# The bias of the own products as a row product on TensorE, and their copy on ScalarE, in the norm stage of a graph and mixture-of-experts kernel

## The chip, the cores and the metric

The kernel runs on one core of a Trainium2 chip. The core has five engines that run their own instruction queues in order: TensorE (PE in the profile, with its weight loads apart as PEld), VectorE (DVE), ScalarE (ACT), GpSimd (POOL) and SyncE (SP, which here only issues transfers). Sixteen DMA engines move data between HBM and the on-chip memory SBUF; matrix products land in PSUM, from which another engine must copy them. The metric is the time of one execution on the device in microseconds (us). Of several executions the median is compared.

## The reference, cut to what matters

```
x = x + gnn(layernorm(x), src, dst, W_self1, W_neigh1, b1, W_self2, W_neigh2, b2)
x = x + moe(layernorm(x), Wg, W1, b1, W2, b2, gamma, beta)

def sage_layer(h, src, dst, W_self, W_neigh, b):
    agg = segment_sum(h[src], dst, n_nodes)
    deg = segment_sum(ones, dst, n_nodes)
    return relu(h @ W_self + (agg / max(deg, 1)) @ W_neigh + b)
```

The graph part is two such layers over 6250 nodes of 512 floats and 100000 edges sorted by target. The mixture-of-experts part picks 2 of 8 experts for each node. Everything is float32. What the change touches is one term of the first layer: `h @ W_self1 + b1`, with h the normed rows; below it is called the own product, and `b1` (the argument `gb1` of the kernel) its bias, a row of 512 numbers.

## The kernel before

Nodes are cut into 49 blocks of 128 rows (the last has 106). The kernel runs in stages: the norm stage (the first 117 us), the first layer with its edge sums, the second layer with its routing, and the experts' end. The edge sums gather rows of the normed matrix `xn_d` from HBM by GpSimd's indirect transfers (`gather`, L216), and the first gather has to wait until the last block is normed and stored.

The norm stage is one loop of 54 steps over k (from L505 on), in an order written out by hand: PE, DVE, ACT and POOL execute their instructions in exactly the order in which the program issues them. In step k:

- `stats` of block k: row statistics on DVE (L460, L462), then a square root on ACT (L464).
- `add_bias` in steps 14, 17, 20, ...: DVE adds the bias, spread over 128 rows in `bb1`, to the own product made five steps before, out of PSUM (L494).
- `nearly`, in steps 9 to 23: DVE copies a turned table of edge indices out of PSUM (L152), whose transposition PE did in the step before.
- `norm` of block k-1: DVE takes the reciprocal and scales the rows (L472, L473), SP stores them to `xn_d` (L476), and PE transposes them into one of three PSUM tiles `pt` (four transposes, L480).
- `turn_edges`, in steps 8 to 22: DVE casts an index table to float (L149) and PE transposes it (L151).
- `keep` of block k-4: ACT copies the transposed block out of PSUM into the resident table `big` (L484). This frees the `pt` tile that `norm` of the same step wants.
- `own` in steps 9, 12, 15, ..., 45 (13 of them): four float32 products of a kept block with `ws1` into a PSUM tile `pm`, of which there are three (L489; the profile counts two passes for each product, so 8).

The own products of the other 36 blocks are made later, in the first layer (`u0`, L561), and are not touched. Their bias is still `bb1`.

GpSimd's queue in this stage holds, in this order: the loads of the edge indices (L141, L143), the experts' rows (`experts_rows`, L380), two small stores, and then the gathers. `experts_rows` loads `b1`, then handles `b2`, `gamma` and `beta` of the experts one after the other: it splits each 8x512 table into three bf16 parts whose sum is the float32 value (load L386, cast L389, store L390, cast back L393, subtract L394) and loads the stored parts again as 24 rows (L395). Each step of this waits for the one before it, since the queue is in order.

Of the kernel before, what the change touches and what calls it, by code (L numbers as in the profile page):

```python
# [29 lines left out]
F32 = mybir.dt.float32  # L30
I32 = mybir.dt.int32
U32 = mybir.dt.uint32
BF16 = mybir.dt.bfloat16
# [16 lines left out]
def bcast(ap, n):  # L50

    return bass.AP(tensor=ap.tensor, offset=ap.offset, ap=[[0, P], [1, n]])
# [15 lines left out]
def gnn_moe(ctx, tc, x, src, dst, Ws1, Wn1, gb1, Ws2, Wn2, gb2, Wg, W1, b1, W2, b2, gamma, beta, out):  # L68
    nc = tc.nc
    N, D = x.shape  # L70
    E = src.shape[0]
    NE = Wg.shape[1]
    C = D // P
# [12 lines left out]
    dram = ctx.enter_context(tc.tile_pool(name="dram", bufs=1, space=DRAM))  # L86
# [20 lines left out]
    ones_h = consts.tile([P, P], BF16, name="ones_h")  # L107
# [218 lines left out]
    def part(i):  # L326
        return big[:, i * D : (i + 1) * D]
# [49 lines left out]
    pick_e = rt.tile([NP3, NE], F32, name="pick_e")  # L377
    thirds = {name: rt.tile([NP3, D], BF16, name=f"{name}_3") for name in ("b2", "gamma", "beta")}

    def experts_rows(pool, psp):  # L380
        b1r = pool.tile([NE * HC, P], F32, name="b1r")
        nc.gpsimd.dma_start(b1r, b1.rearrange("e (c p) -> (e c) p", p=P))
        for name, ap in (("b2", b2), ("gamma", gamma), ("beta", beta)):
            to = dram.tile([NE, 3, D], BF16, name=f"{name}_d")
            left = pool.tile([NE, D], F32, name=f"left_{name}")
            nc.gpsimd.dma_start(left, ap)  # L386
            for k in range(3):
                h = pool.tile([NE, D], BF16, name=f"h_rows{k}")
                nc.gpsimd.tensor_copy(h, left)  # L389
                nc.gpsimd.dma_start(to[:, k], h)  # L390
                if k < 2:
                    f = pool.tile([NE, D], F32, name="f_rows")
                    nc.gpsimd.tensor_copy(f, h)  # L393
                    nc.gpsimd.tensor_sub(left, left, f)  # L394
            nc.gpsimd.dma_start(thirds[name], to.rearrange("e k d -> (e k) d"))  # L395
        lo = pool.tile([NP3, NE], F32, name="lo")
        nc.vector.tensor_scalar(lo, iota_row[:NP3, :NE], 3.0, iota_p[:NP3], op0=OP.mult, op1=OP.subtract)
        hi = pool.tile([NP3, NE], F32, name="hi")
        nc.vector.tensor_scalar(hi, lo, -3.0, None, op0=OP.is_gt)
        nc.vector.tensor_scalar(lo, lo, 0.0, None, op0=OP.is_le)  # L400
        nc.vector.tensor_mul(pick_e, lo, hi)

        def turn():
            pt = psp.tile([P, P], F32, name="pd")
            nc.tensor.transpose(pt[:, : NE * HC], b1r, ident[: NE * HC, : NE * HC])
            nc.vector.tensor_copy(b1T, pt[:, : NE * HC])

        return turn
# [7 lines left out]
    xnT = [part(b).rearrange("p (c n) -> p c n", c=C) for b in range(NB)]  # L416
# [3 lines left out]
    def load_w(w, name):  # L420
        t = lay.tile([P, C, D], F32, name=name)
        nc.scalar.dma_start(t, w.rearrange("(c p) f -> p c f", p=P))
        return t

    def load_b(b, name):
        t = lay.tile([P, D], F32, name=name)
        nc.scalar.dma_start(t, bcast(b, D))
        return t

    with tc.tile_pool(name="l0", bufs=3, side="right") as pool, \  # L430
            tc.tile_pool(name="prep", bufs=1, side="right") as prep, \
            tc.tile_pool(name="l0p", bufs=2, space=PSUM) as psp:

        batch = []
        for lo, hi in ((NS, NB), (0, NS)):
            full = hi if rows[hi - 1] == P else hi - 1
            at = lo
            while at < full:
                batch.append((at, min(4 if batch else 1, full - at)))
                at += batch[-1][1]  # L440
            batch += [(b, 1) for b in range(full, hi)]
        order = [b0 + t for b0, m in batch for t in range(m)]
        at_batch = {b0: i for i, (b0, m) in enumerate(batch)}
        stores = {b0 + m - 1: (b0, m) for b0, m in batch[:-1]}
        stores.update({b: (b, 1) for b in range(batch[-1][0], sum(batch[-1]))})
        where, spread, turned, made = {}, {}, {}, []

        def load(i):
            if i < len(batch):
                b0, m = batch[i]  # L450
                n = rows[b0]
                xt = pool.tile([P, 4, D], F32, name="xt")
                xn = pool.tile([P, 4, D], F32, name="xn")
                nc.sync.dma_start(xt[:n, :m], x[b0 * P : b0 * P + m * n].rearrange("(t p) d -> p t d", p=n))
                where.update({b0 + t: (xt[:, t], xn, t) for t in range(m)})

        def stats(b):
            n = rows[b]
            st = pool.tile([P, 6], F32, name="st")
            nc.vector.bn_stats(st[:n], where[b][0][:n])  # L460
            mv = pool.tile([P, 2], F32, name="mv")
            nc.vector.bn_aggr(mv[:n], st[:n])  # L462
            rs = pool.tile([P, 1], F32, name="rs")
            nc.scalar.activation(rs[:n], mv[:n, 1:2], AF.Sqrt, bias=eps[:n], scale=1.0)  # L464
            spread[b] = mv, rs

        def norm(b):
            n = rows[b]
            mv, rs = spread.pop(b)
            xt, xns, t = where.pop(b)  # L470
            xn = xns[:, t]
            nc.vector.reciprocal(rs[:n], rs[:n])  # L472
            nc.vector.tensor_scalar(xn[:n], xt[:n], mv[:n, 0:1], rs[:n], op0=OP.subtract, op1=OP.mult)  # L473
            if b in stores:
                b0, m = stores[b]
                nc.sync.dma_start(xn_d[b0 * P : b0 * P + m * n].rearrange("(t p) d -> p t d", p=n),  # L476
                                  xns[:n, t + 1 - m : t + 1])
            turned[b] = psp.tile([P, C, P], F32, name="pt", bufs=3)
            for c in range(C):
                nc.tensor.transpose(turned[b][:, c, :n], xn[:n, c * P : (c + 1) * P], ident[:n, :n])  # L480

        def keep(b):
            n = rows[b]
            nc.scalar.activation(xnT[b][:, :, :n], turned.pop(b)[:, :, :n], AF.Copy)  # L484

        def own(b):
            ps = psp.tile([P, D], F32, name="pm", bufs=3)
            for c in range(C):
                nc.tensor.matmul(ps, xnT[b][:, c], ws1[:, c], start=(c == 0), stop=(c == C - 1))  # L489
            made.append((b, ps))  # L490

        def add_bias():
            b, ps = made.pop(0)
            nc.vector.tensor_add(part(b), ps, bb1)  # L494

        load(0)
        load(1)
        dT = prep.tile([P, NCH * TS], F32, name="dT")
        nearly = None
        NE1 = NB - NS  # L500
        when = [9 + j * (NB - 9) // NE1 for j in range(NE1)]
        with tc.manual_schedule(engines=HAND):


            for k in range(NB + 5):  # L505
                if k < NB:
                    if order[k] in at_batch:
                        load(at_batch[order[k]] + 2)
                    stats(order[k])
                if k == 0:  # L510

                    nc.gpsimd.tensor_copy(tick, spread[order[0]][0][:1, :1])
                    raws = load_edges(prep)
                    ws1 = load_w(Ws1, "ws1")
                    bb1 = load_b(gb1, "bb1")
                    turn_b1 = experts_rows(prep, psp)
                    edges_for_loops(prep)
                if k == NB // 2:
                    wn1 = load_w(Wn1, "wn1")
                if k - 5 in when:  # L520
                    add_bias()
                if nearly:
                    nearly()
                    nearly = None
                    if not raws:
                        edge_tables(prep, psp, dT)
                if 0 <= k - 1 < NB:
                    norm(order[k - 1])
                if k >= 8 and raws:
                    nearly = turn_edges(prep, psp, dT, *raws.pop(0))  # L530
                if k == NB // 2:
                    turn_b1()
                if 0 <= k - 4 < NB:
                    keep(order[k - 4])
                if k in when:
                    own(order[when.index(k)])
            while made:
                add_bias()

    lay = b_ctx.enter_context(tc.tile_pool(name="lay2", bufs=1, side="left"))  # L540
    wn2, ws2 = (lay.tile([P, C, D], F32, name=name) for name in ("wn2", "ws2"))
# [358 lines left out]
    with tc.tile_pool(name="s2", bufs=2, side="right") as pool, \  # L900
# [3 lines left out]
        own = {}  # L904
# [295 lines left out]
    def slow_path(pool, psp):  # L1200
# [68 lines left out]
        def spread(name, ap):  # L1269
            t = pool.tile([P, D], F32, name=name)  # L1270
            nc.sync.dma_start(t, bcast(ap, D))
            return t

        def layer(own, wn, ws, bb, b, n, last):
            r = bass.ds(b * P, n)
            a = load_rows("now", agg, r, n)
# [95 lines left out]
```

## Time and profile before

| what | value |
|---|---|
| median of 3 runs | 3350.38 us (3343.76 to 3356.97) |
| the profiled execution | 3328.7 us, its span 3326.4 us |
| busy over the span: PE, DVE, ACT, POOL | 2694.6, 1346.4, 691.5, 1846.9 us |
| mean granted TensorE clock | 0.894 |
| first gather of the first layer (L220) | starts at 117.45 us |
| 20 to 40 us: PE, DVE, ACT busy | 14.23, 12.74, 4.42 us of 20 |
| 80 to 100 us: PE, DVE, ACT busy | 20.00, 19.15, 9.58 us of 20 |
| L494, the addition of the bias | 13 times, 8.6 us in all, 660 ns each |
| L489, the own products | 104 passes, 53.7 us in all |
| L484, ACT's copy of a transposed block | 48 full ones, 27.4 us in all |

The profile shows one execution. A line of its timelines gives the start in us, the length in us, the engine and the line of the program, the operation, the output and the inputs, and how many such instructions were merged into the line; a bracket at its end tells how long the engine had been idle before and what released it. "MATMUL" durations overlap: the next product starts before the one before it has ended.

The span is an unbroken sequence of stages, so what lengthens or shortens the norm stage moves everything behind the first gather.

### The profile page before, as it was taken

To read this page: it belongs to the slowest core of one execution; us is meant where nothing else is said; L and a number is where in the kernel's file an instruction comes from. 1 tells how busy PE (TensorE), PEld (TensorE's weight loads), DVE (VectorE), ACT (ScalarE), POOL (GpSimd) and SP (SyncE) were. 2 spreads that over 40 slices of the span, in tenths; PEclk is the share of its full clock that TensorE was granted. 3 is DMA by queue.
4 is the path that set the end of the run, shared out by engine and by line. 5 is a ranking of instruction groups with operands and counts; after the bars stand their busy time and mean duration, and the time that the engine had idled before them with its cause. 6 is when DMAs were issued, how large, how long until landed. Compare 5 with 4: busy or idle time off the path is not lost. (4 is left out here: it accounts for less than half of the span.)

```text
span 3326.4 us, 34415 instructions
## 1 busy us (share of the span) xinstructions
PE 2694.6 (81%) x10010; PEld 1075.8 (32%) x10010; DVE 1346.4 (40%) x4313; ACT 691.5 (21%) x1261; POOL 1846.9 (56%) x2129
## 2 busy tenths in 40 slices
PE   6768878788887789778747888887888888899995
PEld 3223323233332333223212333332333333344442
DVE  6422222222222222234334454445445454654675
ACT  2211111111111111011112222232222322122221
POOL 4466666666666662666666555555655551650443
PEclk8988988988989899889868888997988998999997
DMA  7767667766776663888877667776766663321696
GB/s 234 229 193 211 205 205 211 226 208 206 217 210 207 198 200 107 268 270 283 269 237 259 220 206 218 221 221 210 222 206 209 216 219 109 129 73 57 217 305 226
DMA packets 266654, 693.41 MB, mean 208 GB/s; under 512 B 42684, under 2 KB 42798, under 8 KB 266428
## 3 DMA queue, kind: packets, MB, share of 16 engines
q0 software_dynamic: 144000, 464.43, 46.4%
q1 hardware_dynamic: 118796, 219.84, 19.2%
q10 hardware_dynamic: 3664, 6.85, 0.6%
q8 instruction: 85, 1.39, 0.2%
q14 instruction: 109, 0.89, 0.1%
HBM read 554.35 MB, written 137.40 MB: 208 GB/s over the span
## 5 line engine op out<-in xcount | busy, mean ns | idle before, releaser
L220 POOL DMA_INDIRECT big<-z,srcT x782 | 748.9, 958 | 584.2 <-PE pa L248 241.8
L220 POOL DMA_INDIRECT rows_t<-xn_d,srcT x782 | 740.5, 947 | 470.2 <-issue 187.5
L559 PE MATMUL pm<-wn,tT 128*128 128x512 f32 x752 | 365.9, 631 | 46.7 <-ACT tT L196 29.1
L826 PE MATMUL ph<-big,xg 128*128 x544 | 312.8, 727 | 79.1 <-DVE y L884 50.1
L860 PE MATMUL py<-w,hT 128*128 x656 | 306.7, 611 | 13.0 <-ACT y L878 8.5
L248 PE MATMUL pa<-big,hot 128*32 128x512 f32 x1564 | 252.0, 662 | 9.9 <-DMA big<-z,srcT 5.9
L248 PE MATMUL pa<-rows_t,hot 128*32 128x512 f32 x1564 | 238.8, 621 | 12.4 <-DMA rows_t<-xn_d,srcT 9.6
L1095 POOL DMA_INDIRECT big<-ys,yrow x98 | 106.9, 1090 | 230.6 <-DMA ys<-y 135.0
L559 PEld LDWEIGHTS pm<-wn,tT 128*128 128x128 f32 x752 | 142.2, 199 | 275.2 <-issue 214.8
L826 PEld LDWEIGHTS ph<-big,xg 128*128 128x128 f32 x544 | 121.5, 235 | 281.2 <-issue 214.2
L290 PE MATMUL ps<-st,sel 128*128 128x512 bf16 (+1 forms) x459 | 139.1, 450 | 47.7 <-issue 38.7
L860 PEld LDWEIGHTS py<-w,hT 128*128 128x128 f32 x656 | 119.3, 192 | 177.9 <-issue 135.9
L925 PE MATMUL ph<-w 128*128 128x512 f32 x288 | 148.8, 665 | 23.4 <-DVE big L1005 17.3
L559 PE MATMUL pm<-ws,big 128*128 128x512 f32 x320 | 153.9, 627 | 0.0
L993 POOL DMA_INDIRECT xs<-big,slot x98 | 98.6, 1006 | 98.1 <-DVE slot L989 43.1
L273 ACT CAST st<-pa 128x512 bf16<-128x512 f32 x132 | 77.3, 586 | 344.3 <-DVE pa L272 211.8
L265 DVE CAST counts<-pn 128x8 bf16<-128x8 f32 x66 | 10.9, 166 | 340.4 <-remote 177.0
L837 DVE TENSOR_SCALAR hT<-pt,b1T 128x128 f32<-128x128 f32 x272 | 76.7, 343 | 177.6 <-PE pt L834 133.0
L290 PEld LDWEIGHTS <-sel 128*128 128x128 bf16 (+1 forms) x918 | 85.7, 107 | 189.9 <-issue 96.5
L1005 DVE SCALAR_TENSOR_TENSOR big<-ph,rcnt,big 128x512 f32<-128x512 f32 (+1 forms) x49 | 36.8, 751 | 266.1 <-PE ph L290 94.0
L1136 PE MATMUL ph<-big,xg 128*128 x296 | 136.9, 605 | 0.0
L290 PE MATMUL ph<-st,sel 128*128 128x512 bf16 (+1 forms) x459 | 120.1, 411 | 17.5 <-DVE sel L280 14.6
(265 smaller groups left out, 3473.8 us busy)
## 6 DMA issues: line engine op xcount, KB each, us to landing
xg<-xs SPq DMA_DIRECT2D x105, 256.0 KB
ys<-y SPq DMA_DIRECT2D x105, 256.0 KB
rows_t<-xn_d,srcT POOLq DMA_INDIRECT x782
big<-z,srcT POOLq DMA_INDIRECT x782
z<-big SPq DMA_DIRECT2D x48, 256.0 KB
xa<-in_x SPq DMA_DIRECT2D x48, 256.0 KB
big<-s SPq DMA_DIRECT2D x48, 256.0 KB
accs<-xa SPq DMA_DIRECT2D x48, 256.0 KB
```

The source lines that it names most:

```text
L220: nc.gpsimd.indirect_dma_start(out=gathered[t], out_offset=None, in_=z[:, :], in_offset=bass.IndirectOffsetOnAxis(ap=srcT[:, t : t + 1], a ...
L248: nc.tensor.matmul(pa[0][q * SW : (q + 1) * SW], hots[i][:, q], gathered.pop(t), start=(j == 0), stop=(j == TS - 1 or t == NT_E - 1), tile ...
L273: nc.scalar.copy(st[1][:k], pa[:k])
L290: nc.tensor.matmul(ps, sel[:k], st[h][:k], start=(g == a and h == 0), stop=(g == z and h == 2))
L559: nc.tensor.matmul(ph, tT[:, c], w[:, c], start=(start and c == 0), stop=(stop and c == C - 1))
L826: nc.tensor.matmul(ph, self.xT[:, c], w1[:, bass.ds(self.e * KD + c * D, D)], start=(c == 0), stop=(c == C - 1))
L837: nc.vector.tensor_scalar(hT[:, c], pt[:, c], b1T[:, bass.ds(self.e * HC + c, 1)], 0.0, op0=OP.add, op1=OP.max)
L860: nc.tensor.matmul(self.py, self.hT[:, c], w2[:, bass.ds(self.e * KD + c * D, D)], start=(c == 0), stop=False)
L925: nc.tensor.matmul(ps, hT[:, c], ws2[:, c], start=(c == 0), stop=(c == C - 1))
L993: inst = nc.gpsimd.indirect_dma_start(out=xs[:, :], out_offset=bass.IndirectOffsetOnAxis(ap=slot[:n, b, k : k + 1], axis=0), in_=t["xn"][: ...
L1095: nc.gpsimd.indirect_dma_start(out=yk[:n], out_offset=None, in_=ys[: ready[0] * P, :], in_offset=bass.IndirectOffsetOnAxis(ap=yrow[:n, b, ...
L1136: nc.tensor.matmul(ph, u.xT[:, c], w1[:, bass.ds(u.e * KD + c * D, D)], start=(c == 0), stop=(c == C - 1))
```

## The change

Three things are changed.

- The bias row `gb1` is split into three bf16 parts by the same steps as the experts' rows, in a function made from the body of `experts_rows`, and loaded as a tile `own_bias` of 3 rows. This stands ahead of `experts_rows` in GpSimd's queue: one load, three casts and stores, two casts back, two subtractions and the load of the result.
- `own` gets a fifth product: 3 rows of ones (bf16) times `own_bias`, added into the same PSUM tile. It ends the accumulation.
- `add_bias` on DVE becomes `keep_own`, a plain copy out of PSUM on ACT, and is called three steps after `own` in place of five. In its step it stands between the square root of `stats` and the copy of `keep`.

```diff
+    def thirds_of(pool, name, ap, n):
+
+        to = dram.tile([n, 3, D], BF16, name=f"{name}_d")
+        left = pool.tile([n, D], F32, name=f"left_{name}")
+        nc.gpsimd.dma_start(left, ap)
+        for k in range(3):
+            h = pool.tile([NE, D], BF16, name=f"h_rows{k}")[:n]
+            nc.gpsimd.tensor_copy(h, left)
+            nc.gpsimd.dma_start(to[:, k], h)
+            if k < 2:
+                f = pool.tile([NE, D], F32, name="f_rows")[:n]
+                nc.gpsimd.tensor_copy(f, h)
+                nc.gpsimd.tensor_sub(left, left, f)
+        return to.rearrange("e k d -> (e k) d")
...
-            nc.gpsimd.dma_start(thirds[name], to.rearrange("e k d -> (e k) d"))
+            nc.gpsimd.dma_start(thirds[name], thirds_of(pool, name, ap, NE))
...
         def own(b):
             ps = psp.tile([P, D], F32, name="pm", bufs=3)
             for c in range(C):
-                nc.tensor.matmul(ps, xnT[b][:, c], ws1[:, c], start=(c == 0), stop=(c == C - 1))
+                nc.tensor.matmul(ps, xnT[b][:, c], ws1[:, c], start=(c == 0), stop=False)
+            nc.tensor.matmul(ps, ones_h[:3], own_bias, start=False, stop=True)
             made.append((b, ps))
 
-        def add_bias():
+        def keep_own():
             b, ps = made.pop(0)
-            nc.vector.tensor_add(part(b), ps, bb1)
+            nc.scalar.copy(part(b), ps)
...
+        own_bias = prep.tile([3, D], BF16, name="own_bias")
...
                     bb1 = load_b(gb1, "bb1")
+                    nc.gpsimd.dma_start(own_bias, thirds_of(prep, "own", gb1.rearrange("(o d) -> o d", o=1), 1))
                     turn_b1 = experts_rows(prep, psp)
...
-                if k - 5 in when:
-                    add_bias()
+                if k - 3 in when:
+                    keep_own()
...
             while made:
-                add_bias()
+                keep_own()
```

More of the change, by code (lines that the diff above doesn't have):

```diff
@@ L383, in experts_rows @@
         for name, ap in (("b2", b2), ("gamma", gamma), ("beta", beta)):
[L384 to L395, printed above, removed]
+            nc.gpsimd.dma_start(thirds[name], thirds_of(pool, name, ap, NE))
         lo = pool.tile([NP3, NE], F32, name="lo")
```

## The prediction

> **What bounds the kernel now.** I read the busy shares by stretches first, then the timelines of PE, ACT, DVE and GpSimd over the norm stage. Two stretches of 5 us (busy us of PE, PEld, DVE, ACT and POOL, then clock, DMA share, GB/s):
>
> ```profile
> 85.00:90.00 5.00, 5.00 (x21) 2.77 (x20) 4.79 (x15) 2.39 (x7) 0.00 (x0) 1.00 0.96 320
> 90.00:95.00 5.00, 5.00 (x21) 2.77 (x20) 4.79 (x15) 2.41 (x7) 0.00 (x0) 1.00 0.97 295
> ```
>
> From 75 us on, PE is never idle and DVE hardly. Both are full at once, so relieving DVE alone can't shorten this part. PE's timeline, a group of three steps:
>
> ```profile
> 79.45 3.60 PE L489 MATMUL pm<-ws,big 128*128 128x512 f32 x8
> 82.89 1.65 PE L480 MATMUL pt<-ident,xn 128*128 128x128 f32 x12
> 84.38 3.60 PE L489 MATMUL pm<-ws,big 128*128 128x512 f32 x8
> ...
> 83.88 0.66 PE L480 MATMUL pt<-ident,xn 128*128 128x128 f32 x4
> ```
>
> A group lasts 84.38 - 79.45 = 4.93 us: 3.44 for the eight passes, 1.49 for twelve transposes. The last line (the same view, cut at 84) shows where the third block's transposes start: 83.88. What released them is on ACT:
>
> ```profile
> 83.05 0.30 ACT L464 ACTIVATE rs<-mv,eps 128x1 f32<-128x1 f32 x1 [1.27 <-DVE rs L472]
> 83.25 0.58 ACT L484 ACTIVATE big<-pt 128x512 f32<-128x512 f32 x1
> ...
> 112.91 2.53 ACT L484 ACTIVATE big<-pt 128x512 f32<-128x512 f32 x5
> ```
>
> The copy ends at 83.83 and frees the `pt` tile; PE starts 0.05 later. So ACT, half idle, is already on the path by that one copy. Five copies in a row take 2.53 us: (2.53 - 0.62) / 4 = 0.48 from start to start, 0.62 being the last of them.
>
> Before 75 us it is a chain of single steps, DVE to PE and back, with PE's own products inside it:
>
> ```profile
> 22.38 4.70 PE L489 MATMUL pm<-ws,big 128*128 128x512 f32 x8
> 26.92 0.60 PE L480 MATMUL pt<-ident,xn 128*128 128x128 f32 x4
> ...
> 31.66 1.09 PE L480 MATMUL pt<-ident,xn 128*128 128x128 f32 x4 [1.40 <-DVE f L149]
> ...
> 27.66 0.29 DVE L152 COPY dT<-pd 128x128 f32<-128x128 f32 x1 [3.14 <-PE pd L151]
> ```
>
> DVE waits 3.14 us for PE's first own product. Last, GpSimd's queue, from the end of the index loads to the first gather:
>
> ```profile
> 16.62 0.62 POOL L382 DMA_DIRECT2D b1r<-in_L_ffn_b  x1 [0.25 <-DMA raw_d<-in_dst]
> 17.24 0.51 POOL L386 DMA_DIRECT2D left_b<-in_L_ffn_b  x1
> 22.21 0.60 POOL L389 CAST h_rows<-left_b 8x512 bf16<-8x512 f32 x1 [4.47 <-DMA left_b<-in_L_ffn_b]
> ...
> 32.54 0.53 POOL L395 DMA_DIRECT2D b<-b_d  x1 [1.95 <-DMA b_d<-h_rows]
> 33.06 0.51 POOL L386 DMA_DIRECT2D left_gamma<-in_L_ffn_gamma  x1
> 39.72 0.60 POOL L389 CAST h_rows<-left_gamma 8x512 bf16<-8x512 f32 x1 [6.15 <-DMA left_gamma<-in_L_ffn_gamma]
> ...
> 117.45 1.06 POOL L220 DMA_INDIRECT rows_t<-xn_d,srcT  x1 [47.11 <-DVE hot L230]
> ```
>
> Splitting one table takes 17.24 to 32.54 = 15.30 us. GpSimd then idles 47 us, so its own lateness costs the gathers nothing. What matters is who needs the result.
>
> **The change, part by part.**
>
> *The row arrives late.* The new split takes the place of `b1r` in the queue and starts at 16.62. With the rows of `b2` (casts of 512 columns, one partition in place of eight; I assume no difference) its final load is issued at 16.62 + 15.30 = 31.92. Its landing: the nearest quiet row is the third store of `b_d`, issued at 30.07 and waited for until 32.54, 2.47 us; the nearest loads took 33.06 to 39.72 = 6.66 and 17.24 to 22.21 = 4.97, under row blocks being loaded. I take 2.47, because the loads of blocks wait for DVE, which stands still here. So 34.4. PE needs it at 26.92, in the fifth product of the first own product, and its queue is in order: transposes, index transposes, then DVE's copy at L152, the next `norm` and ACT behind it all wait. Cost 34.4 - 26.9 = 7.5, all on the path. Low 5.5, if the short first load takes 3 us in place of 4.97; high 11.7, with 6.66 for the last one.
>
> *What the stall leaves.* After it PE may run at half clock. Four transposes take 0.60 at 26.92 and 1.09 at 31.66, where the clock was halved; an index transpose 0.27 and 0.42. Three steps up to the next own product, each dearer by about 0.5, are 1.5; one was slow before: 1.0. Low 0 (after the idle 64.90 to 68.34 the transposes still took 0.63), high 2.0. The Trainium skill (TensorE: Matmul & The Clock Gate, Part 1: The HAM clock gate) says that an idle window of some 3.4 us returns PE to half clock, which speaks against this change. By it the term would be 1.5, the total 0.5 more; the row at 68.34 doesn't bear it out.
>
> *ACT's copy ahead of `keep`, to 75 us.* In steps 12, 15, 18, 21 and 24 `keep` ends 0.48 later. The transposes that need it had a slack of 0.11, 0.20, 0.20, 0.13 and 0 us (ACT's copies end at 31.50, 40.61, 50.04, 57.74, 72.12 and the transposes start at 31.66, 40.86, 50.28, 57.92, 72.17, less 0.05 for the handover). Left: 1.8. Between 0 (if DVE is later still) and 5 x 0.48 = 2.4.
>
> *The fifth product.* Nearest row, a bf16 row product of the same width over 24 rows:
>
> ```profile
> L854 PE MATMUL py<-b,its x105: 384/385/605, 1806.7 to 3286.0; 24*128 24x512 bf16 x105
> ```
>
> 384 ns to its end; the next product starts 0.23 after it. Four own products before 75 us (the first is in the stall) give 4 x 0.23 = 0.9, up to 2.0 at half clock with the weight load bare.
>
> *DVE's addition removed.* Thirteen times 0.57 between starts. To 75 us three lie in DVE's wait for PE (34.81, 44.63, 52.88) and are worth nothing; at 68.93 it is on the path: -0.6. From 75 us on nine are off a DVE that is no longer the bound, and the last (113.88) comes after all norms. Were DVE the bound, they would be -5.1.
>
> *The groups from 75 us.* Let an own product start at X. Its eighth pass is followed at X + 3.44 by the row product, done at X + 3.82; ACT starts `keep_own` at X + 3.86, `keep` 0.48 later at X + 4.34, which ends at X + 4.92; PE transposes from X + 4.97 and starts the next own product 0.50 later, at X + 5.47. Before, it was X + 4.93: 0.54 more, in six groups from 79.45 to 109.09, 3.2. The first (73.46 to 79.45), partly at half clock, gets about 0.8. Together 4.0. If `keep_own` found another gap, PE's 0.23 less its present wait of 0.13 remains, 0.1 x 7 = 0.7; with two handovers of 0.05 more in each of the seven, 4.7 at the high end. Behind ACT's wait for the own product stand `keep`, the next square root and so DVE's next reciprocal; PE's transposes are late next.
>
> *The end of the stage.* DVE now runs ahead of PE and its last norm no longer sets the last store; PE's last transposes gate the gathers (they wait for PE, ACT and the stores). Before, the gather came 8.36 after the last own product began (109.09): 6.96 to about 116.05, where the last store had landed, and 1.40 behind it. Now ACT's next `keep`, 0.48 behind the one above, ends at X + 5.40, the last block's four transposes end at about X + 6.1, and the gather comes at X + 7.5: -0.9. Bounds -2.4 (the stores alone gate, landing at about X + 4.5) and 0.
>
> *Nothing for the rest.* The experts' rows end some 16 us later, near 86, before 117; `b1r` is issued at about 32.5 and wanted at 73. With their cover gone each would cost its own lateness.
>
> Sum: 7.5 + 1.0 + 1.8 + 0.9 - 0.6 + 4.0 - 0.9 = 13.7 us. Low ends: 5.5 + 0 + 0 + 0.9 - 0.6 + 0.7 - 2.4 = 4.1; high: 11.7 + 2.0 + 2.4 + 2.0 - 0.6 + 4.7 = 22.2. The profiled execution would take 3328.7 + 13.7 = 3342.4 with a span of 3340.1. It was 21.7 below the median of the runs, so for the median I add to 3350.4: **3364.1**.
>
> **The rivals.**
>
> *Slower beyond doubt.* One mechanism: the row's last load meets a burst of block loads and takes 6.66 us, as `left_gamma` did. Then the stall is 11.7, and the sum 17.9: 3368.3. For: all three loads of this kind waited 4.5 to 6.2 us. Against: those bursts are released by DVE. It decides from a landing later than some 38 us.
>
> *DVE sets the pace.* The row is in time and ACT finds room: 0.9 for the row products, -0.6 - 5.1: 3345.6. For: DVE is 96% busy from 75 us. Against: PE has no gap to run faster in, and the row can't be split before 26.9 by any row shown.
>
> *The clock.* The granted clock averages 0.894; PE is busy 2694.6 us, so 0.01 of it is worth some 30 us. A shift of the stage can move half-clock windows either way: 3335 or 3390. Against: nothing in the change touches PE's later work.
>
> **How the numbers follow.** 0.5% of the median is 16.75 us, about what a measurement of this kernel can tell from no change: faster is below 3333.6, slower above 3367.1. Forecast 0.48, the late landing 0.38, DVE's pace 0.06, the clock 0.04 each way. So faster 0.04, same 0.54, slower 0.42. Range: 3350.4 + 4.1 less the runs' spread of 6.6, to 3350.4 + 22.2 and 6.6: 3348 to 3379. The forecast's own is 3357 to 3367.
>
> **What would show it.** PE idle 7 us behind the first own product, released by the transfer of `own_bias`; DVE's copy at L152 late by the same; groups of 5.4 to 5.5 us from 80 us on, with ACT's copies in pairs; the first gather near 131. Wrong if groups take 4.9 or less, if the product at 26.9 finds its row there, or if the gather is late and the end isn't.

## The result and the profile after

Twenty runs of each kernel: the median is 3359.51 us (3350.82 to 3387.04) after the change and 3346.9 us (3325.33 to 3366.84) before it. The ratio is 1.0042 with a 95% interval of 1.0023 to 1.0062: slower, by 7.7 to 20.8 us. The ratio itself is inside the 0.5% that the prediction called no change; the upper end of its interval is not. The prediction had added 13.7 us; the ratio says 14.1, the two medians 12.6, and the stage below says more. Of the 4.6 us between the forecast of 3364.1 and the median, 3.5 belong to the kernel before, whose median over twenty runs is lower than the 3350.4 that the forecast was counted from.

The profiled execution spans 3359.6 us. Its lines stand against those shown of before. GpSimd's timeline after the change:

```profile
16.60 0.60 POOL L384 DMA_DIRECT2D left_own<-in_L_gnn_b  x1 [0.24 <-DMA raw_d<-in_dst]
21.57 0.60 POOL L387 CAST h_rows<-left_own 1x512 bf16<-1x512 f32 x1 [4.38 <-DMA left_own<-in_L_gnn_b]
...
29.29 0.50 POOL L388 DMA_DIRECT2D own_d<-h_rows  x1 [0.29 <-POOL h_rows L387]
32.31 0.52 POOL L522 DMA_DIRECT2D own_bias<-own_d  x1 [2.52 <-DMA own_d<-h_rows]
...
135.27 1.15 POOL L220 DMA_INDIRECT rows_t<-xn_d,srcT  x1 [52.47 <-ACT big L488]
```

The split takes 16.60 to 32.31, 15.71 us, where the one of `b2` took 15.30 before: one partition is as slow as eight. The first gather starts at 135.27 in place of 117.45: the stage is 17.8 us longer. PE's timeline at the first own product, and DVE's next instruction that waits for it:

```profile
22.33 5.49 PE L493 MATMUL pm<-ws,big 128*128 128x512 f32 x8
34.03 0.58 PE L494 MATMUL pm<-own_bias,ones_h 3*128 3x512 bf16 x1 [6.21 <-DMA own_bias<-own_d]
34.54 1.11 PE L484 MATMUL pt<-ident,xn 128*128 128x128 f32 x4
...
37.00 1.09 PE L484 MATMUL pt<-ident,xn 128*128 128x128 f32 x4 [1.13 <-DVE f L149]
...
35.91 0.29 DVE L152 COPY dT<-pd 128x128 f32<-128x128 f32 x1 [10.05 <-PE pd L151]
```

PE stands for 6.21 us until the row lands, DVE for 10.05, and the transposes behind take 1.1 in place of 0.6; the granted clock was 0.50 in 35 to 40 us. A group from 80 us on, on PE and then on ACT:

```profile
94.24 3.60 PE L493 MATMUL pm<-ws,big 128*128 128x512 f32 x8
97.77 0.39 PE L494 MATMUL pm<-own_bias,ones_h 3*128 3x512 bf16 x1
98.09 1.09 PE L484 MATMUL pt<-ident,xn 128*128 128x128 f32 x8
99.39 0.66 PE L484 MATMUL pt<-ident,xn 128*128 128x128 f32 x4 [0.21 <-ACT big L488]
99.88 3.60 PE L493 MATMUL pm<-ws,big 128*128 128x512 f32 x8
...
98.25 0.59 ACT L499 COPY big<-pm 128x512 f32<-128x512 f32 x1 [2.45 <-PE pm L494]
98.73 0.60 ACT L488 ACTIVATE big<-pt 128x512 f32<-128x512 f32 x1
```

Groups last 99.88 - 94.24 = 5.64 us, 4.94 before. ACT idles 2.45 us for the own product, copies it, copies the transposed block 0.48 behind, and only when that ends does PE go on. In 95 to 100 us DVE is no longer full (3.61 us of 5, 4.79 in the stretches before), and neither is PE (4.79, 5.00 before; columns as there):

```profile
95.00:100.00 5.00, 4.79 (x21) 2.51 (x20) 3.61 (x12) 2.08 (x7) 0.00 (x0) 1.00 0.92 263
```

Where the 17.8 us came from, by the starts of the own products (L489 before, L493 after) and the first gather, in us:

| stretch | before | after | more |
|---|---|---|---|
| start to the 1st own product | 22.38 | 22.33 | 0.0 |
| 1st to 2nd | 10.37 | 18.19 | 7.8 |
| 2nd to 6th | 40.71 | 45.57 | 4.9 |
| 6th to 7th | 5.99 | 8.15 | 2.2 |
| 7th to 13th, six groups | 29.64 | 33.84 | 4.2 |
| 13th to the first gather | 8.36 | 7.19 | -1.2 |

Behind the first gather, the two profiled executions differ by 15.3 us more (3208.95 against 3224.23). That is within the spread of the later stages: a second profile of the same changed kernel, below, took 3210.3 there. So single spans say little about some 10 us here, and the experiments are read by the first gather, which moved by 0.9 us between those two profiles.

### The profile page after: what moved, and what is told of

It is laid out like the page before. It is cut to its first block, busy times and chain, and to the rows that moved or that the text cites. A ratio compares the mean times of both kernels' runs of the same rounds, so it can differ in the third digit from the quotient of the medians.

```text
span 3359.6 us, 34372 instructions
## 1 busy us (share of the span) xinstructions
PE 2701.7 (80%) x9927; PEld 1082.1 (32%) x10023; DVE 1339.4 (40%) x4300; ACT 697.4 (21%) x1274; POOL 1855.3 (55%) x2141
## 3 DMA queue, kind: packets, MB, share of 16 engines
q0 software_dynamic: 144160, 464.44, 45.9%
## 5 line engine op out<-in xcount | busy, mean ns | idle before, releaser
L248 PE MATMUL pa<-big,hot 128*32 128x512 f32 x1564 | 259.6, 664 | 17.2 <-DMA big<-z,srcT 9.8
L290 PE MATMUL ps<-st,sel 128*128 128x512 bf16 x411 | 120.8, 435 | 37.7 <-issue 35.9
L274 DVE TENSOR_TENSOR st<-pa,st 128x512 bf16<-128x512 f32 x132 | 91.2, 691 | 87.9 <-ACT st L273 52.4
```

The lines of the kernel that those rows point to most:

```text
L248: nc.tensor.matmul(pa[0][q * SW : (q + 1) * SW], hots[i][:, q], gathered.pop(t), start=(j == 0), stop=(j == TS - 1 or t == NT_E - 1), tile ...
L274: nc.vector.tensor_sub(st[2][:k], pa[:k], st[1][:k])
L290: nc.tensor.matmul(ps, sel[:k], st[h][:k], start=(g == a and h == 0), stop=(g == z and h == 2))
```

## The experiments

Each run is compared by its first gather (117.45 before, 135.27 after) and by the time of a group.

**The row at hand.**

```diff
-                    nc.gpsimd.dma_start(own_bias, thirds_of(prep, "own", gb1.rearrange("(o d) -> o d", o=1), 1))
+                    nc.gpsimd.memset(own_bias, 0.0)
```

> The changed kernel with the three rows of own_bias set to zero by GpSimd at 16.6 us in place of the split and its load, so the bias is left out of the 13 own products of the norm stage; row product and ScalarE copies stay. If the lateness of the row is the largest term, the distance from the first to the second own product falls from 18.2 us to about 10.7, the first gather comes at 126 to 128 us (135.3 with the split, 117.5 before), and the whole is within 0.4% of the kernel before (ratio about 1.003). If the row product and the copies cost the early steps as much as the late row does, the first gather stays behind 132 us.

Measured: first gather 127.05, groups 5.64, the first own product 10.81 from the second. The whole: 1.0045 (1.0021 to 1.0068), more than the 1.003 expected; its interval holds both the 9.6 us of the stage and the changed kernel's 17.8. So the late row, with the slow steps behind it, is 135.27 - 127.05 = 8.2 us of the stage (9.1 against the second profile), 7.4 of them between the first and the second own product; the whole run can't show it. The other 9.6 come from the row product and the copies.

**The split, unused.** The kernel before, with

```diff
+                    nc.gpsimd.dma_start(own_bias, thirds_of(prep, "own", gb1.rearrange("(o d) -> o d", o=1), 1))
                     turn_b1 = experts_rows(prep, psp)
```

> The kernel before with the split of the row in GpSimd's queue at the place it has in the changed kernel, but with nobody using its result; VectorE adds the bias as before. If a longer queue of GpSimd costs nothing by itself, the first gather stays at 117.5 us within 1. If GpSimd's longer work slows VectorE beside it or the transfers, it moves to 119.5 us or later.

Measured: first gather 116.82, groups 4.94. GpSimd's longer work and its lateness cost the stage nothing here; what is left as the price of the split is the wait for its result.

**The copies behind keep.** The changed kernel with

```diff
-                if k - 3 in when:
-                    keep_own()
...
                 if 0 <= k - 4 < NB:
                     keep(order[k - 4])
+                if k - 3 in when:
+                    keep_own()
```

> The changed kernel with keep_own called behind keep in its step, not ahead of it. If ScalarE's copy ahead of keep is what stretches the groups, they fall from 5.64 us to 5.0 to 5.1 (VectorE's and TensorE's work alone), the early groups lose some 0.4 each, and the first gather comes at 129 to 131 us. If the wait for the own product merely moves to the square root behind it and stops VectorE there, groups stay at 5.4 us or more and the gather behind 133.

Measured: first gather 129.54, groups 5.21. PE's timeline of this run:

```profile
96.73 3.60 PE L493 MATMUL pm<-ws,big 128*128 128x512 f32 x8
100.26 0.38 PE L494 MATMUL pm<-own_bias,ones_h 3*128 3x512 bf16 x1
100.57 1.53 PE L484 MATMUL pt<-ident,xn 128*128 128x128 f32 x12
101.94 3.60 PE L493 MATMUL pm<-ws,big 128*128 128x512 f32 x8
```

No idle bracket is left: PE alone bounds the group. So ACT's place in the order cost 0.43 a group and 5.7 us of the stage. But the group was expected at 5.0 to 5.1: the row product starts 100.26 - 96.73 = 3.53 after the own product, not 3.44, and holds PE for 0.31.

**The changed kernel again.**

> The changed kernel once more, as a measure of how much the stage varies: first gather at 135.3 us within 1.5, groups of 5.64 us within 0.05, the row's product at 34.0 us within 1.

Measured: first gather 136.14, groups 5.64, the row's product at 34.51. The difference to the first profile lies in the early steps, where the first gap is 18.66 against 18.19.

**The row at hand and the copies behind.** Both edits above.

> Zeros in place of the split (the bias is left out of the 13 own products) and keep_own behind keep: what is left of the change is the row product and ScalarE's copies in a place where nothing waits for them. If TensorE bounds the groups there, they last 5.21 us as with the copies behind alone, of which the row product is 0.41 (0.10 bare ahead of it and 0.31 after its start), and the first gather comes at 121 to 124 us. If the copies on ScalarE still cost something, groups stay above 5.3.

Measured: first gather 121.31, groups 5.21. Taking out the late row and the handover removes 14.0 of the 17.8 us. The 3.9 left are the row product's cost less what relieving DVE gains: the last version below, which does the same without the row product, reaches its first gather at 113.82, so the row product costs 7.5 us of the stage.

**The copies alone.** ScalarE copies ahead of `keep`; split and row product are taken out.

```diff
-                nc.tensor.matmul(ps, xnT[b][:, c], ws1[:, c], start=(c == 0), stop=False)
-            nc.tensor.matmul(ps, ones_h[:3], own_bias, start=False, stop=True)
+                nc.tensor.matmul(ps, xnT[b][:, c], ws1[:, c], start=(c == 0), stop=(c == C - 1))
```

> ScalarE's copies ahead of keep as in the changed kernel, but without the row product and without the split (the bias is left out of the 13 own products). If the handover own product, copy, keep, transposes sets the groups, they last 5.2 to 5.3 us even without the fifth product, and the first gather comes at 121 to 124 us. If the row product was the cause, groups go back to 4.9 and the gather to 118 or less.

Measured: first gather 120.95, groups 5.32. PE's timeline shows who ends the group:

```profile
98.11 3.60 PE L493 MATMUL pm<-ws,big 128*128 128x512 f32 x8
101.55 1.04 PE L484 MATMUL pt<-ident,xn 128*128 128x128 f32 x8
102.94 0.66 PE L484 MATMUL pt<-ident,xn 128*128 128x128 f32 x4 [0.36 <-ACT big L488]
```

The third block waits for ACT's copy even without the fifth product. Adding that product lengthens this chain by 5.64 - 5.32 = 0.32.

**The row product alone.** Zeros at hand, and VectorE copies in the old place.

```diff
-            nc.scalar.copy(part(b), ps)
+            nc.vector.tensor_copy(part(b), ps)
...
-                if k - 3 in when:
+                if k - 5 in when:
```

> The row product with zeros at hand, copied out by VectorE five steps later, where the addition was (the bias is left out of the 13 own products). If the row product costs TensorE 0.41 us in each group, groups last 5.2 us with VectorE waiting a little, and the first gather comes at 121 to 123 us. If VectorE still sets the pace or the product costs 0.23 as predicted, groups last 4.9 to 5.1 and the gather comes at 118 to 120.

Measured: first gather 122.83, groups 5.21. The product costs what PE loses to it, whoever copies. Of the 5.4 us more than before, six groups hold 1.6. The stretch from the second to the sixth own product holds 4.7 (45.38 against 40.71), 3.6 of it between the fourth and the fifth, where PE was at half clock for longer (that own product took 5.02 in place of 3.60). The group ahead of the six adds 0.8, and the end of the stage gives 1.6 back.

**The split in full, begun in time.** Copies behind `keep`, and the own products from step 14 on.

```diff
-        when = [9 + j * (NB - 9) // NE1 for j in range(NE1)]
+        when = [14 + j * (NB - 14) // NE1 for j in range(NE1)]
```

> The changed kernel with two edits: keep_own behind keep, and the 13 own products begun in step 14 and not in step 9 (2 or 3 steps apart), so that the split row is there when first wanted. The bias is in. If the late row costs only by TensorE waiting for it, no wait for own_bias is left and the first gather comes at 120 to 123 us, like the run with zeros at hand and the copies behind (121.3), though the split is made in full. If the split's transfers slow the stage by themselves, it comes at 126 us or later.

Measured: first gather 122.47. GpSimd's and PE's timelines of this run:

```profile
30.37 0.50 POOL L388 DMA_DIRECT2D own_d<-h_rows  x1 [0.29 <-POOL h_rows L387]
36.95 0.52 POOL L522 DMA_DIRECT2D own_bias<-own_d  x1 [6.08 <-DMA own_d<-h_rows]
...
35.56 5.86 PE L493 MATMUL pm<-ws,big 128*128 128x512 f32 x8
41.98 0.37 PE L494 MATMUL pm<-own_bias,ones_h 3*128 3x512 bf16 x1 [0.56 <-DMA own_bias<-own_d]
```

The stage is within 1.2 us of that with zeros at hand (121.31), so the late row's cost is, as far as these runs tell, PE's wait; the own products also stand closer together here. That wait was not quite gone: 0.56 is left. The row lands near 42 here, not at 34. DVE doesn't stand still, SP issues the next block loads at 29.64 and 32.07 (in the changed kernel only at 39.31), and the DMA engines were busy for 1.00 of 35 to 40 us, against 0.06 of 30 to 35 us in the changed kernel.

**A version meant to beat both.** No split and no row product; ScalarE copies behind `keep`, and VectorE adds the bias later, where it is far from full.

```diff
+            def plus_bias():
+                nc.vector.tensor_add(part(b), part(b), bb1)
...
-            return ([(1, "post", u0)] if b < NS else []) + [
+            return [(1, "post", u0 if b < NS else plus_bias)] + [
```

> A version meant to beat both: no split, no row product; ScalarE copies the own product out behind keep, and VectorE adds the bias in the first layer, in SBUF, one slot after the block's sum. If TensorE bounds the groups, they last 4.8 to 4.9 us (4.94 before), the stage ends by the transposes, and the first gather comes at 115 to 116 us (117.5 before); the whole moves by 2 us at most, which these runs can't tell from no change (ratio within 0.3% of 1). If the additions moved to the first layer cost there, the first layer is longer by up to 13 x 0.7 = 9 us.

Measured: first gather 113.82, groups 4.75, ratio 0.9976 (0.9949 to 1.0004). PE's timeline:

```profile
93.19 3.60 PE L493 MATMUL pm<-ws,big 128*128 128x512 f32 x8
96.63 1.47 PE L484 MATMUL pt<-ident,xn 128*128 128x128 f32 x12
97.94 2.31 PE L493 MATMUL pm<-ws,big 128*128 128x512 f32 x5
```

PE runs without a gap: 3.44 for the own product and 1.31 for twelve transposes. Both group and first gather came out below what was expected, and they show who set the pace before. There DVE's timeline has no idle time between 75 and 113 us, and its additions follow each other at the length of a group, 95.71 - 90.77 = 4.94 (the kernel before):

```profile
90.77 0.66 DVE L494 TENSOR_TENSOR big<-pm,bb 128x512 f32<-128x512 f32 x1
...
95.71 0.66 DVE L494 TENSOR_TENSOR big<-pm,bb 128x512 f32<-128x512 f32 x1
```

PE's own work is 4.75, so PE had 0.19 to spare in each group before. Its busy share of 5.00 doesn't show that, since the "MATMUL" lengths overlap. Relieving DVE, with the copy on ACT where nothing waits for it, is worth that 0.19. Once more, with more runs:

> The version with the bias added by VectorE in the first layer, once more and with more rounds: groups 4.75 us and the first gather at 113.8 us within 1; the whole 0.1% under the kernel before by the stage's 3.6 us, so a ratio of 0.997 to 1.001. If the 0.9976 of the first runs was the version itself and not the spread, the ratio is 0.997 to 0.998 again.

Measured: first gather 112.97, groups 4.75, ratio 1.0 (0.9978 to 1.0022). The stage is 3.6 to 4.5 us shorter than before. The whole shows no difference from the kernel before that these runs could tell, and whether the 13 additions (8.8 us of DVE in the first layer, none with idle time ahead of it) cost anything there stays open: from the first to the last gather of that layer the two profiles took 1156.5 and 1177.2 us, and the kernel before 1162.6.

## Why the prediction was right, and where it was not

*The late row* (7.5, and 1.0 for what it leaves): right in place, and near in size. The row was used at 34.03; predicted was 34.4. Taking it out gave 8.2 us, with the copies ahead of `keep` and with the copies behind, where 8.5 was said. The parts were each off. The own product ahead of the row took 5.49 us and not 4.70, so PE waited 6.21; against the runs with zeros at hand the row's product came 5.9 and 6.7 later (28.18 to 34.03, 27.34 to 33.99 with the copies behind), not 7.5. The slow steps behind it cost 1.5 and 1.4, not 1.0. That the sum came out so near is in part luck.

The reason given for the short landing, that block loads wait for DVE, which stands still, agrees with the run begun later, where DVE went on and the row landed at 42. That landing was the mechanism of the rival "slower beyond doubt"; in the changed kernel the stall protects its own transfer.

*Half clock behind the stall*: three steps of transposes at 1.1 us, as said. I weighed the Trainium skill (TensorE: Matmul & The Clock Gate, Part 1: The HAM clock gate), by which an idle window of some 3.4 us returns PE to half clock, against one row and took a middle value. The transposes after the 6.21 us of idle time agree with the page. The row at 68.34 is no evidence against it: an idle gap of 3.43 to 3.51 us stands at that place in eleven of the twelve profiles, and the four transposes behind it took 0.63 us in five, 0.81 in one and 1.07 to 1.09 in five. In these runs a gap of that length went either way.

*The fifth product*: the step that was mis-sized, "the next product starts 0.23 after it". With nothing else in the way, a group without it lasts 4.75 us and with it 5.21: 0.46. The trace of before held both cases; 0.23 is the distance to another row product, and 0.31 the distance to transposes, which follow here (the kernel before):

```profile
1806.67 0.38 PE L854 MATMUL py<-b,its 24*128 24x512 bf16 x1
1806.98 0.66 PE L834 MATMUL pt<-ident,h 128*128 128x128 f32 x4
...
2852.64 0.39 PE L854 MATMUL py<-b,its 24*128 24x512 bf16 x1
2852.87 0.37 PE L854 MATMUL pg<-gamma,its 24*128 24x512 bf16 x1
```

Besides, 0.09 ahead of the product (3.53 in place of 3.44) and 0.06 at the transposes that follow were left out. This is also why the groups came to 5.64 and not to 5.47: the row product started 0.09 later, and its end and the handovers took the remaining 0.08. Six groups cost 4.2 where 3.2 was said, and the group ahead of them 2.2 where 0.8 was said, since it also ran at half clock for longer.

*ACT's copy ahead of `keep`*: right as a mechanism. It is shown from both sides, by the copies alone (5.32, PE idle 0.36 for ACT) and by the copies behind (no idle left). Its size is 5.7 us of the stage, in the changed kernel (135.27 to 129.54) and with zeros at hand (127.05 to 121.31). The prediction had 1.8 for the early steps and 3.3 for the groups (4.0 less the 0.7 that another gap leaves): 5.1.

*The early steps*: here the prediction was furthest off. From the second to the sixth own product it had 1.4 of ACT's 1.8 (0.4 lies ahead of the second), 0.9 for the fifth product and -0.6 for the addition: 1.7 where 4.9 was measured. The term that failed is the fifth product again. This stretch took 42.9 to 45.9 us in the six runs that have the row product and begin in step 9, and 39.4 to 42.1 in the five without it. In the pairs that differ there by the product (in the first also by a copy on DVE for the addition), it cost 3.5 to 4.7 (row product alone against before, row at hand against copies alone, row at hand and copies behind against both runs of the last version); 0.9 was said, 2.0 at most. Of that, 4 x 0.46 = 1.8 is the price seen in the groups. What the rest is stays open. The granted clock over this stretch was 0.77 to 0.82 with the row product and 0.79 to 0.87 without, but one pair with nearly the same clock (0.80 and 0.79) still differs by 3.7.

*The removed addition*: "relieving DVE alone can't shorten this part" was wrong by 0.19 a group, as the version with the bias added later shows; in the changed kernel the row product takes more from PE than that. The -0.6 in one place was not tried by itself. *The end of the stage*: -1.2 measured, -0.9 predicted. *Nothing for GpSimd's longer queue*: shown (116.82).

Taken apart step by step, the changed kernel's 135.27 less 5.7 for the place of ACT's copy, 8.2 for the late row and 7.5 for the row product is the 113.82 of the version without them, and the 3.6 up to 117.45 are what the move off DVE gained. By the prediction's own terms the run with zeros at hand and the copies behind would have been about 0.9 - 0.6 + 0.7 - 0.9 = 0.1 us longer than before; it was 3.9 longer, and that is most of what the forecast lacks.

So the stage grew by 17.8 to 18.7 us and not by 13.7. The ratio's interval holds both, and the ratio fell on the near side, which is luck. The forecast, no change that can be told at 0.5%, holds by the ratio, with the stage's own growth just over the 16.75 us of that bound. The rival "slower beyond doubt" had 17.9 us, nearly what the stage grew by, but by a landing after 38 us that did not come. The rival in which DVE sets the pace fails as it stood: DVE did set the pace, by 0.19 a group, but relieved of its addition it stood idle, for PE's work is next. Of the rival by the clock nothing was seen: the granted clock of the twenty changed runs was 0.892 to 0.901, against 0.894 in the profile of before.

## What to carry to other kernels

Before work is moved off a busy engine, look whether the engine it waits for, or the one it is moved to, is already on the same path: here PE's own work was 4.75 of a group's 4.94 us and one ACT copy already released it, so taking 0.57 us off DVE could buy 0.19, and the 0.46 put on PE and the 0.48 put on ACT cost far more. In a queue that runs in order, a copy that waits for a late product belongs behind the copies that somebody else waits for. And a constant made by a chain of small transfers is late by the whole chain for its first user; either start the users later or add it where it is not in the way.

## What the runs showed of the hardware that was not expected

- A bf16 product of three rows among float32 products of full size costs PE 0.46 us, twice the 0.23 from one row product to the next: it starts 0.09 late (its weight load, 0.09 long, is recorded at 100.25 in the run with the copies behind, the product itself at 100.26), the next transposes start 0.31 behind it, and they take 0.06 more.
- GpSimd's casts and subtractions of 512 columns took about the same time on one partition (0.60 and 1.25 to 1.32 us after the change) as on eight (0.60 to 0.69 and 1.25 to 1.26 before).
- The same 1 KB store, waited for at the end of the split, took 2.52 us beyond its issue when the DMA engines were busy for 0.06 of 30 to 35 us (after the change), and 6.08 when they were busy for 0.78 of it and 1.00 of the next 5 us (the split begun in time).
